# A one-core attention and expert kernel: three more filler matmuls, the last copies in another order, and each expert weight loaded in four column pieces

## The chip, the cores and the metric

The kernel runs on one core of a Trainium2 chip. Its engines are TensorE (PE, matrix multiplication), VectorE (DVE), ScalarE (ACT), GpSimd (POOL) and SyncE (SP, which here only issues DMAs). The metric is device time in microseconds, the median of several executions. Beside these there is one profiled execution, whose trace gives the time of every instruction and, in windows, the clock that PE was granted (1.00 is full speed).

## The reference, cut to what matters

The input is an image of 256 channels on 48 x 48 positions, that is 2304 tokens. Two layers run over it, each with a residual. The second half of layer 1 is the part that the change touches.

```python
# layer 0: group norm, then softmax attention over 2304 tokens x 4 heads in one sequence of 9216
x = x + conv_attn(group_norm(x))          # softmax(q k^T / 8) v, q/k/v: 9216 x 64
# layer 1
t = tokens(x)                              # 2304 x 256
t = t + slice_attn(layer_norm(t))          # 64 slices, 8 heads
t = t + ffn(layer_norm(t))
out = image(t)                             # back to 1 x 256 x 48 x 48

def ffn(xf):                               # 8 experts, each token goes to 2 of them
    top_w, top_i = top_k(xf @ Wg + bg, 2);  top_w = softmax(top_w)
    w_dense = sum(one_hot(top_i, 8) * top_w[..., None], axis=1)
    for e in range(8):
        h = gelu(xf @ W1[e] + b1[e])       # 256 -> 1024
        out = out + w_dense[:, e:e+1] * (h @ W2[e] + b2[e])   # 1024 -> 256
    return out
```

## The kernel before, in words

**Order of the whole.** Layer 0's attention takes the first 1211 us and isn't touched. Slice attention follows, to about 1248 us; then routing, to about 1277 us; then the expert tiles, to about 1568 us; then the end, which adds the last tile and writes the output. A second copy of all layers stands behind a condition at the end of the program; it handles rare inputs and is not run here. It is built from the same function, `layers(tc, bad, ...)` with `bad=None`.

**What sets the order.** `pe`, `dve`, `act`, `pool` and `sp` are wrappers (`InOrder`, L65 to 76) that keep every instruction on its engine in the order in which it is written; since the wrapper issues them, most instructions carry line 73 in the profile and are told apart by the names of their tiles. Between engines a framework puts in semaphores: a reader waits for the writer of the part of a tile that it reads, and a writer of a buffer waits until its last readers are done. Indirect DMAs on POOL are kept in written order by `indirect` (L1314 in the profile). DMAs of W1 are issued by SP directly (L1354).

**Routing (L1120 to L1266).** DVE computes each token's two experts and its slot: tokens are sorted by expert and cut into tiles of 128 slots, each tile of one expert. To invert the map (which token sits in a slot?) PE multiplies one-hot matrices: `find_rows(k, n)` has DVE write n one-hot planes and PE accumulate n matmuls of 43 columns into `pw`. There are 36 of them, in groups of 6, 12, 12 and 6. Between the groups PE waits for DVE. The transpose `pex` brings out the expert of each tile. `pq` then spreads the positions for gathers in quarters. Where PE would have nothing to do, `busy(n, bank)` (L458) issues n matmuls of 256 columns whose result nobody reads (`spin<-Wqkv_sb,ident` in the profile; each fp32 matmul leaves two records). Thirteen of them stand before the one-hot groups, three after them and seven at the end. The very next PE work then waits for the first gather of tokens.

**Expert tiles.** There are 39 tiles here: first tiles 36, 37 and 38 (`near`), then 0 to 35 (`SURE` is 36); further ones (`rare`) are not run. For tile s:

- `parts` or `rows` gathers its 128 token rows with indirect DMAs on POOL, three tiles ahead; `turn` or `turn_parts` transposes them into `xT`.
- `load_w1(s, w1)` (L1352) reads the tile's expert number into an SP register and loads the whole W1 of that expert, 1 MB, into one of two buffers of 128 partitions x 2 x 1024. It stands two tiles ahead: the load of s+2 is issued after `first(s)`, and since it writes the buffer that `first(s)` reads, it waits for `first(s)` to be done.
- `first(s)` (L1401) makes 16 matmuls into `ph`: for each of the eight blocks f of 128 hidden columns two (c = 0, 1) over the two halves of the 256 inputs, with `w1[:, c, f*128 : (f+1)*128]` as PE's weights. ACT applies gelu block by block.
- `second(s)` (L1419) multiplies with W2, which lies in SBUF (`w2_sb`): 8 matmuls into `py`; DVE adds the bias and multiplies with the routing weight (`y`). `first` of a tile stands ahead of `second` of the tile before.
- `scatter` adds y to the tokens `t_d` in DRAM by an indirect DMA on POOL.

**The end (L1599 to L1634).** The 2304 output tokens are cut into five blocks: 0 and 1 (tokens 1792 on and 1280 on, 512 each, `EARLY`), which the last two tiles cannot reach, are loaded while these tiles run; 2 (768, 512 tokens), 3 (0, 512) and 4 (512, 256) are loaded after the last scatter (`LATE`). For each block and each half c of the channels, `columns(b, c)` transposes on PE into a PSUM bank out of the ring of three `ph` banks; `finish(b, c)` (L1534) copies it to SBUF: c = 0 on DVE, c = 1 on ACT, followed by the block's output DMA, issued by ACT for blocks 0, 1 and 4 and by SP for the others. A bank can be written again only when its copy is done. The last tile, 35, is not scattered: DVE splits its y into three bf16 parts (`thirds`, five DVE instructions), and PE adds them to the blocks 2 to 4 by three one-hot matmuls (`here`) on top of the transposes. In the order of before, the copies of block 0 stand after `second(35)` and those of block 1 after the split into `thirds`.

Of the kernel before, what the change touches and what calls it, by code (L numbers as in the profile page):

```python
# [18 lines left out]
P = 128  # L19
# [15 lines left out]
HID = 1024  # L35
# [43 lines left out]
def layers(  # L79
# [10 lines left out]
    nc = tc.nc  # L90
# [3 lines left out]
    pe, dve, act, pool = (InOrder(tc, e) for e in (nc.tensor, nc.vector, nc.scalar, nc.gpsimd))  # L94
# [18 lines left out]
        out=not_before, in_=not_before, pattern=[[-1, P]], compare_op=ALU.is_ge,  # L113
# [69 lines left out]
    for c, pieces in enumerate(((1152, 1152), (1152, 768, 384))):  # L183
# [10 lines left out]
        out=gmat, in_=gmat, pattern=[[-8, 16], [0, 8]], compare_op=ALU.is_ge,  # L194
# [3 lines left out]
        out=gmat, in_=gmat, pattern=[[8, 16], [0, 8]], compare_op=ALU.is_ge,  # L198
# [37 lines left out]
    def load_rows(src, n, name):  # L236
        t = const.tile([P, 2, n], FP, name=name)
        nc.sync.dma_start(out=t, in_=src.rearrange("(c p) n -> p c n", p=P))
        return t
# [3 lines left out]
    Wqkv_sb = load_rows(Wqkv, 3 * C, "Wqkv_sb")  # L243
# [3 lines left out]
    for h in range(H1):  # L247
        at = ((h // 2) % 2 * 2 + h // 4) * D1
        nc.sync.dma_start(
            out=Wout_sb[at : at + D1, h % 2, 0:C], in_=Wout[h * D1 : (h + 1) * D1, :]  # L250
# [38 lines left out]
    with proj, tc.tile_pool(name="ps_pj", bufs=5, space=PSUM) as ps_pj, tc.tile_pool(  # L289
# [147 lines left out]
        for i in range(NTT):  # L437
            pv = ps_pj.tile([P, 512], FP, name="pp", tag="pp")
            for c in range(2):
                nc.tensor.matmul(  # L440
                    pv[:, 0:C], xn[:, c, i * P : (i + 1) * P], WvT[:, c, :],
                    start=(c == 0), stop=(c == 1),
# [15 lines left out]
    def busy(n, bank):  # L458

        for _ in range(n):  # L460
            pe.matmul(bank[:, 0:256], ident, Wqkv_sb[:, 0, 0:256], start=True, stop=True)
# [146 lines left out]
    def attention():  # L608
# [220 lines left out]
    spin = idle.enter_context(tc.tile_pool(name="ps_spin", bufs=1, space=PSUM)).tile(  # L829
        [P, 256], FP, name="spin"  # L830
    )
# [27 lines left out]
    for c in range(2):  # L859
        pe.matmul(  # L860
            pts[:, c, :], sums_of[:, c * P : (c + 1) * P], fold.rearrange("p a s -> p (a s)"),
            start=(c == 0), stop=False,
# [10 lines left out]
    for ci in range(2):  # L873
        for k in range(2):
            pe.matmul(
                gates[:, ci, :], turned[:, k, ci * P : (ci + 1) * P], Wl[:, k, S : S + E],
                start=(k == 0), stop=(k == 1),
            )
    for k in range(2):
        pe.matmul(  # L880
            gates[:, 2, :], bcol[:, B_OUT + k : B_OUT + k + 1].to_broadcast([P, P]), Wl[:, k, S : S + E],
            start=(k == 0), stop=(k == 1),
# [3 lines left out]
    for c in range(2):  # L886
        for i in range(NTT - 2, NTT):
# [3 lines left out]
                start=False, stop=(c == 1 and i == NTT - 1),  # L891
# [25 lines left out]
    with tc.tile_pool(name="sa", bufs=1) as sa, sums_done, tc.tile_pool(  # L917
# [10 lines left out]
        with tc.tile_pool(name="ps_b", bufs=3, space=PSUM) as ps_b:  # L928
# [5 lines left out]
            for m in range(2):  # L934
                for c in range(2):
                    pe.matmul(
                        ph[:, m, :], W0_sb[:, c, m * P : (m + 1) * P], ts_sum[:, c * S : (c + 2) * S],
                        start=(c == 0), stop=(c == 1),
# [28 lines left out]
            for u in range(2):  # L967
                ph = ps_b.tile([P, 2, 2 * S], FP, name="ph", tag="mm")
                phs.append(ph)
                for kind in range(2):  # L970
                    j = 2 * kind + u
                    for c in range(2):
# [3 lines left out]
                            start=(c == 0), stop=(c == 1),  # L976
# [57 lines left out]
            pt = ps_b.tile([P, 2, S], FP, name="pt2", tag="mm")  # L1034
# [8 lines left out]
            for w in range(2):  # L1043
                pe.matmul(
                    pw, tokT[:, w].rearrange("p a s -> p (a s)"), Wout_sb[:, w, :],
                    start=(w == 0), stop=(w == 1),
# [23 lines left out]
        with tc.tile_pool(name="ps_y0", bufs=1, space=PSUM) as ps_y0:  # L1070
# [3 lines left out]
            for g, (i0, n) in enumerate(groups):  # L1074
                pys = [next(banks)[:, 0 : C + E] for _ in range(n)]
                for i in range(i0, i0 + n, 4):
                    some = range(i, min(i + 4, i0 + n))
                    for k in some:
# [4 lines left out]
                            stop=(k < 4 or k in by_dve),  # L1083
# [4 lines left out]
                for k, py in enumerate(pys):  # L1088
# [16 lines left out]
                    out=t_d[(i0 + 1) * P : (i0 + n + 1) * P, :].rearrange("(i p) c -> p i c", p=P),  # L1105
                    in_=t_sb[:, these, 0:C],
# [13 lines left out]
    with gating, tc.tile_pool(name="onehot", bufs=1) as oh, tc.tile_pool(  # L1120
# [68 lines left out]
        for k in range(2):  # L1189
# [4 lines left out]
            out=tn_d[P : P + NT, C : C + E].rearrange("(i p) e -> p i e", p=P), in_=w_e  # L1194
# [15 lines left out]
        dve.scalar_tensor_tensor(row, first_slot, -BIG, slot, ALU.add, ALU.subtract)  # L1210

        which = oh.tile([P, NSL, K], HF, name="which")
        in_row = t_flat.bitcast(HF)[:, 0 : P * K].rearrange("p (r k) -> p r k", k=K)
        in_tile = t_flat.bitcast(HF)[:, P * K : (P + NSL) * K].rearrange("p (n k) -> p n k", k=K)
        pw = ps_lg.tile([P, NSL], FP, name="pw")
        pex = ps_lg.tile([1, P], FP, name="pex")
        busy(13, spin)
        tokens = token.rearrange("p k i -> p (k i)")
        dve.tensor_tensor(
            in_tile, tile_of.unsqueeze(1).to_broadcast([P, NSL, K]), tile_tab, ALU.is_equal  # L1220
        )
        def weigh(k):
            ks = slice(k, k + NTT)
            dve.tensor_tensor(
                which[:, :, ks], in_tile[:, :, ks],
                tokens[:, ks].unsqueeze(1).to_broadcast([P, NSL, NTT]), ALU.mult,
            )

        def find_rows(k, n):
            dve.tensor_tensor(  # L1230
                in_row[:, :, k : k + n], row[:, k : k + n].unsqueeze(1).to_broadcast([P, P, n]),
                row_tab[:, :, k : k + n], ALU.is_equal,
            )
            for j in range(k, k + n):
                pe.matmul(pw, in_row[:, :, j], which[:, :, j], start=(j == 0), stop=(j == K - 1))
# [6 lines left out]
        dve.tensor_reduce(ex, past, AX.X, ALU.add)  # L1242
        dve.tensor_copy(used_i, ends[0:1, E - 1 : E])
        pe.transpose(pex, ex, ident)
        find_rows(6, 12)
        dve.tensor_copy(expert_i, pex[:, 0:NSL])
        weigh(NTT)
        find_rows(NTT, 12)
# [19 lines left out]
    def expert_of(s, engine):  # L1268
        return nc.values_load(
            expert_i[:, s : s + 1], engines=(engine,), min_val=0, max_val=E - 1,  # L1270
            skip_runtime_bounds_check_because="it is counted from 0 and cut at E - 1",
        )

    idle.close()
    with tc.tile_pool(name="ps_h", bufs=1, space=PSUM) as ps_h, tc.tile_pool(
# [75 lines left out]

        def load_w1(s, w1):  # L1352
            e = expert_of(s, mybir.EngineType.SP)
            nc.sync.dma_start(  # L1354
                out=w1, in_=W1[bass.ds(e, 1)].rearrange("e (p c) f -> p (e c) f", p=P)
            )
            return w1

        def behind(ins, last):
# [59 lines left out]
        def second(s, hid, meanwhile):  # L1419

            e = expert_of(s, mybir.EngineType.PE)
            py = next(ring_py)
            for f in range(NHC):
                pe.matmul(
                    py, hid[:, f, :],
                    w2_sb[:, bass.ds(e, 1), f, :].rearrange("p e d -> p (e d)"),
                    start=(f == 0), stop=(f == NHC - 1),
                )
                if f == 2:
                    meanwhile()  # L1430
            e = expert_of(s, mybir.EngineType.DVE)
            y = next(ring_y)
            dve.tensor_tensor(
                y, py, b2_e[:, bass.ds(e, 1), :].rearrange("p e d -> p (e d)"), ALU.add
            )
            dve.tensor_scalar(y, y, slot_w.pop(s), None, ALU.mult)
            return y
# [14 lines left out]
        xs, w1, xT, hid, slot_w = {}, {}, {}, {}, {}  # L1452
        for s in near:
            xs[s] = rows(s, next(near_xs))
        for s in range(2):
            w1[SURE + s] = load_w1(SURE + s, next(ring_w1))
# [31 lines left out]
        turn_next(SURE)  # L1488
        hid[SURE] = first(SURE, xT.pop(SURE), w1.pop(SURE))
        w1[SURE + 2] = load_w1(SURE + 2, next(ring_w1))  # L1490
        scatter(SURE, second(SURE, hid.pop(SURE), more_turns))
        used = nc.values_load(
# [22 lines left out]
        blocks, pts, ob_of = [], {}, {}  # L1515
# [8 lines left out]
        def columns(b, c):  # L1524
            t0, n, tt = blocks[b]
            pts[b, c] = next(ring_ph).rearrange("p a b -> p (a b)")
            by_row = pts[b, c][:, 0:n].rearrange("q (p k) -> q k p", p=P)
            for k in range(n // P):
                pe.matmul(
                    by_row[:, k, :], tt[:, k, c * P : (c + 1) * P], ident, start=(k == 0),  # L1530
                    stop=(t0 >= reach and k == n // P - 1), is_transpose=True,
                )

        def finish(b, c):  # L1534
            t0, n, _ = blocks[b]
            pt = pts.pop((b, c))
            if c == 0:
                ob_of[b] = next(obs)
                dve.tensor_copy(ob_of[b][:, c, 0:n], pt[:, 0:n])
            else:  # L1540
                act.copy(ob_of[b][:, c, 0:n], pt[:, 0:n])

                queue = act if t0 in (1792, 1280, 512) else sp
                queue.dma_start(out=out_v[:, :, t0 : t0 + n], in_=ob_of.pop(b)[:, :, 0:n])
# [3 lines left out]
        for s in range(SURE):  # L1548
# [41 lines left out]
            if 8 <= s < 8 + len(TBLOCKS):  # L1590
                t0, n = TBLOCKS[s - 8]
# [9 lines left out]
        if bad is not None:  # L1601
            columns(0, 0)
            columns(0, 1)
        y = second(SURE - 1, hid.pop(SURE - 1), lambda: None)
        if bad is not None:
            columns(1, 0)
            finish(0, 0)
            finish(0, 1)
            columns(1, 1)
            busy(2, next(ring_py))  # L1610
        else:
            busy(4, next(ring_py))
# [4 lines left out]
        dve.tensor_copy(thirds[:, 2], rest[:, 1])  # L1617
        first_late = 0
        if bad is not None:
            finish(1, 0)  # L1620
            finish(1, 1)
            first_late = 2
        todo = [(b, c) for b in range(first_late, len(blocks)) for c in range(2)]
        columns(*todo[0])
        for at, (b, c) in enumerate(todo):
            if at + 1 < len(todo):
                columns(*todo[at + 1])
            t0, n, _ = blocks[b]
            for k in range(3 if t0 < reach else 0):
                pe.matmul(  # L1630
                    pts[b, c][:, 0:n], thirds[:, k, c * P : (c + 1) * P], here[:, t0 : t0 + n],
                    start=False, stop=(k == 2),
# [4 lines left out]
@with_exitstack  # L1637
def kernel(ctx: ExitStack, tc: tile.TileContext, *args):
    nc = tc.nc
    out_v = args[-1][0].rearrange("(c p) h w -> p c (h w)", p=P)  # L1640
    known = ctx.enter_context(tc.tile_pool(name="known", bufs=1))
    bad = known.tile([1, 1], mybir.dt.int32, name="bad")
    ident = known.tile([P, P], FP, name="ident")
    make_identity(nc, ident)
    dram = ctx.enter_context(tc.tile_pool(name="t", bufs=1, space=bass.MemoryType.DRAM))
    t_d = dram.tile([NT + P, C], FP, name="t_d")
    layers(tc, bad, ident, t_d, out_v, *args[:-1])

    flags, (again,) = nc.values_load_multi_w_load_instructions(
        bad, min_val=0, max_val=1, skip_runtime_bounds_check_because="it is the result of a comparison"  # L1650
    )
    for flag in flags:
        tc.keep_in_program_order(flag)
    with tc.If(again > 0):
        layers(tc, None, ident, t_d, out_v, *args[:-1])
# [35 lines left out]
```

## Time and profile before

| what | us |
|---|---|
| median of 3 runs (lowest to highest) | 1576.4 (1575.71 to 1576.87) |
| the profiled execution's own time | 1585.12 |
| its span in the trace | 1583.4 |
| PE busy, of the span | 1558.1 (98%) |
| DVE busy | 1051.8 (66%) |
| ACT busy | 820.9 (52%) |
| POOL busy | 264.9 (17%) |
| mean granted PE clock of the profiled execution | 0.995 |

The profile is of one execution, and it took 8.7 us longer than the median of the runs. A share of busy time is an average over stages; what bounds a stage is read from the stage itself, by the idle time before a group and by what ended it (in brackets, with an arrow from the instruction that was waited for). In a line of a group, the tiles are written as result<-operands, then partitions x elements and the type, then how many instructions there are. A fp32 matmul leaves two or more records; counts of records are not counts of calls. Times in the trace are counted from the start of the span.

### The profile page before, as it was taken

The numbers are of one execution on the slowest core, as the hardware profiler recorded it, in microseconds if no ns is written. First come the engines' busy times: TensorE is split into PE (matmuls) and PEld (weight loads), VectorE is DVE, ScalarE is ACT, GpSimd is POOL, SyncE is SP. The second block draws the span as 40 slices with busy tenths as digits, with TensorE's granted clock in tenths as the row PEclk, the third lists the DMA queues.
The fourth block names the chain that finished last, engine by engine and source line by source line (L and its number), as shares of the span: only waits on it lengthen the run. The fifth ranks groups of instructions, "written<-read, shape, count | busy, mean of one in ns | idle before, by whom it ended". The sixth has DMA issues, their size and how long they took to land. (4 is left out here: it accounts for less than half of the span.)

```text
span 1583.4 us, 32366 instructions
## 1 busy us (share of the span) xinstructions
PE 1558.1 (98%) x13058; PEld 775.6 (49%) x13059; DVE 1051.8 (66%) x1430; ACT 820.9 (52%) x1132; POOL 264.9 (17%) x206
## 2 busy tenths in 40 slices
PE   9999999999999999999999999999999999999997
PEld 5633343333333333333333333333334788899986
DVE  7578777787787877878778778777787712222222
ACT  3356665565665665556556656566654423233322
POOL 1101101011011010110100101101010145656661
PEclk9999999999999999999999999999999989999999
DMA  4000000000000000000000000000001956666656
GB/s 142 2 1 1 1 1 4 5 1 1 8 1 1 8 1 1 8 2 1 6 4 1 2 7 1 1 8 1 1 2 45 317 172 188 169 179 190 180 168 185
DMA packets 57214, 80.08 MB, mean 51 GB/s; under 512 B 27375, under 2 KB 47550, under 8 KB 51934
## 3 DMA queue, kind: packets, MB, share of 16 engines
q1 hardware_dynamic: 47026, 66.01, 12.8%
q0 software_dynamic: 9104, 10.53, 3.7%
q8 instruction: 107, 1.75, 0.5%
q10 hardware_dynamic: 924, 1.35, 0.2%
q14 instruction: 53, 0.43, 0.1%
HBM read 63.37 MB, written 12.40 MB: 48 GB/s over the span
## 5 line engine op out<-in xcount | busy, mean ns | idle before, releaser
L73 DVE TENSOR_TENSOR acc<-acc,p 128x1024 f32<-128x1024 f32 x612 | 749.2, 1224 | 242.7 <-ACT p L73 236.9
L73 ACT ACTIVATE p<-s 128x1024 f32<-128x1024 f32 x648 | 662.8, 1023 | 469.7 <-PE s L73 467.2
L73 PE MATMUL av<-p,v_sb 64*64 64x512 f32 x5184 | 675.8, 590 | 2.5 <-ACT p L73 1.4
L73 PE MATMUL s<-q,kk 64*64 64x512 f32 x5184 | 674.8, 589 | 0.5 <-DVE v_sb L444 0.5
L73 PEld LDWEIGHTS s<-q,kk 64*64 64x64 f32 x5184 | 202.1, 133 | 353.5 <-issue 181.5
L73 PEld LDWEIGHTS av<-p,v_sb 64*64 64x64 f32 x5184 | 195.7, 131 | 358.0 <-ACT p L73 201.1
L73 POOL PARTITION_ALL_REDUCE total<-both x17 | 71.5, 4206 | 954.8 <-ACT p L73 893.4
L73 ACT ACTIVATE hid<-ph,bcol 128x128 f32<-128x128 f32 x312 | 88.8, 369 | 215.4 <-PE ph L73 121.6
L73 PE MATMUL ph<-xT,w 128*128 128x128 f32 x1248 | 146.8, 275 | 4.0 <-issue 1.7
L73 PE MATMUL py<-w_sb,hid 128*128 x624 | 146.9, 383 | 2.9 <-issue 2.5
L73 PEld LDWEIGHTS ph<-xT,w 128*128 128x128 f32 x1248 | 145.8, 192 | 6.8 <-ACTq L1505 2.1
L73 DVE TENSOR_TENSOR y<-py,b_bc 128x256 f32<-128x256 f32 x39 | 16.6, 425 | 172.0 <-PE py L73 102.6
L73 PEld LDWEIGHTS py<-w_sb,hid 128*128 128x128 f32 x624 | 115.3, 192 | 19.4 <-issue 5.2
L1314 POOL DMA_INDIRECT xs<-tn_d,part_t x88 | 90.0, 1023 | 33.6 <-issue 25.9
L1314 POOL DMA_INDIRECT t_d<-y,slot_t x36 | 57.8, 1605 | 78.6 <-DVE xT L73 28.0
L73 DVE COPY xT<-pt 128x256 f32<-128x256 f32 x17 | 7.2, 423 | 50.1 <-PE pt L73 47.1
L73 DVE RECIPROCAL rinv<-rinv 128x256 f32<-128x256 f32 x17 | 29.7, 1745 | 0.0
L73 POOL TENSOR_TENSOR rstd_t<-ve,mhalf 128x2 f32<-128x2 f32 (+2 forms) x13 | 11.0, 848 | 103.4 <-DVE ve L73 96.5
L73 DVE TENSOR_TENSOR acc<-p 128x1024 f32<-128x1024 f32 x18 | 22.8, 1268 | 4.7 <-ACT p L73 3.1
L395 DVE TENSOR_SCALAR q<-pp,bcol 64x512 f32<-64x512 f32 (+1 forms) x30 | 20.8, 694 | 5.0 <-PE pp L378 4.7
L73 DVE TENSOR_REDUCE up<-av 128x512 f32<-128x1024 f32 x17 | 20.8, 1225 | 5.0 <-PE av L73 5.0
L73 PE MATMUL spin<-Wqkv_sb,ident 128*128 128x256 f32 x88 | 24.1, 430 | 0.0
(325 smaller groups left out, 612.6 us busy)
## 6 DMA issues: line engine op xcount, KB each, us to landing
w<-in_L_ffn_W_dram SPq DMA_DIRECT2D x39, 1024.0 KB
w_sb<-in_L_ffn_W_dram SPq DMA_DIRECT2D x8, 1024.0 KB
t_sb<-turned SPq DMA_DIRECT2D x224, 8.0 KB
t_sb<-t_d SPq DMA_DIRECT2D x4, 512.0 KB
x_sb<-in_x_dram SPq DMA_DIRECT2D x3, 576.0 KB
t_d<-t_sb SPq DMA_DIRECT2D x2, 768.0 KB
tn_d<-tn SPq DMA_DIRECT2D x2, 768.0 KB
xs<-tn_d,part_t POOLq DMA_INDIRECT x88
```

Source lines behind the costliest of these rows:

```text
L73: return self.tc.keep_in_program_order(getattr(self.engine, name)(*args, **kwargs))
L395: nc.vector.tensor_scalar(dst, pq[rows, 0:tn], bcol[rows, B_Q + m : B_Q + m + 1], 0.125, ALU.add, ALU.mult,)
L1314: new = nc.gpsimd.indirect_dma_start(**kwargs)
```

## The change

Three things are edited.

- In routing, three fillers are added, each between two one-hot groups: `busy_half()`, new, a matmul of 128 columns, after the thirteen fillers; one `busy(1)` of 256 columns after the transpose `pex`; and a second `busy_half()` after the group `find_rows(6, 12)`.
- `load_w1` issues four DMAs instead of one. Each takes a quarter of the hidden columns (256 of 1024) of both input halves, for all 128 partitions, so that a run in memory is 1 KB and there are 256 runs for each DMA. Each piece waits only for the readers of its own columns, and `first` waits for each piece at f = 0, 2, 4 and 6.
- At the end, `finish(0, 0)` and `finish(0, 1)` go ahead of `second(35)`. After it come `columns(1, 0)` and `columns(1, 1)`, then `finish(1, 0)`, now copied by ACT, and `finish(1, 1)`; all these stand ahead of the split into `thirds`.

The fallback copy gets the fillers and the W1 pieces too, and isn't run.

```diff
         pex = ps_lg.tile([1, P], FP, name="pex")
         busy(13, spin)
+        busy_half()          # pe.matmul(spin[:, 0:P], ident, Wqkv_sb[:, 0, 0:P], start=True, stop=True)
         tokens = token.rearrange("p k i -> p (k i)")
...
         pe.transpose(pex, ex, ident)
+        busy(1, spin)
         find_rows(6, 12)
+        busy_half()
         dve.tensor_copy(expert_i, pex[:, 0:NSL])
...
             e = expert_of(s, mybir.EngineType.SP)
-            nc.sync.dma_start(
-                out=w1, in_=W1[bass.ds(e, 1)].rearrange("e (p c) f -> p (e c) f", p=P)
-            )
+            for f0 in range(0, HID, HID // 4):
+                fs = slice(f0, f0 + HID // 4)
+                nc.sync.dma_start(
+                    out=w1[:, :, fs],
+                    in_=W1[bass.ds(e, 1)].rearrange("e (p c) f -> p (e c) f", p=P)[:, :, fs],
+                )
             return w1
...
-        def finish(b, c):
+        def finish(b, c, by=None):
...
-                dve.tensor_copy(ob_of[b][:, c, 0:n], pt[:, 0:n])
+                (dve.tensor_copy if by is None else act.copy)(ob_of[b][:, c, 0:n], pt[:, 0:n])
...
             columns(0, 1)
+            finish(0, 0)
+            finish(0, 1)
         y = second(SURE - 1, hid.pop(SURE - 1), lambda: None)
         if bad is not None:
             columns(1, 0)
-            finish(0, 0)
-            finish(0, 1)
             columns(1, 1)
+            finish(1, 0, act)
+            finish(1, 1)
             busy(2, next(ring_py))
...
         dve.tensor_copy(thirds[:, 2], rest[:, 1])
         first_late = 0
         if bad is not None:
-            finish(1, 0)
-            finish(1, 1)
             first_late = 2
```

More of the change, by code (lines that the diff above doesn't have):

```diff
@@ L1212, in layers, with busy_half @@
         which = oh.tile([P, NSL, K], HF, name="which")
+        def busy_half():
+            pe.matmul(spin[:, 0:P], ident, Wqkv_sb[:, 0, 0:P], start=True, stop=True)
         in_row = t_flat.bitcast(HF)[:, 0 : P * K].rearrange("p (r k) -> p r k", k=K)
```

## Prediction

> **What bounds the kernel now.** I read the page first, then the clock and busy time by stretch, the order of time at the three places that the change touches, and the weight loads.
>
> ```profile
> PE 1558.1 (98%) x13058; PEld 775.6 (49%) x13059; DVE 1051.8 (66%) x1430; ACT 820.9 (52%) x1132; POOL 264.9 (17%) x206
> PE   9999999999999999999999999999999999999997
> PEclk9999999999999999999999999999999989999999
> ```
>
> TensorE (PE) is the bound almost everywhere: 25 us of the span are not matmul, 7 of them after the last matmul. Only idle PE, or PE at a low clock, can be won. The one 8 in the row of the granted clock lies at the routing stage, between attention and the expert tiles. By stretches of 3.41 us (start and end, length, then the engines, the clock after POOL):
>
> ```profile
> 1259.15:1262.56 3.41, 3.41 (x17) 2.87 (x16) 3.24 (x8) 1.89 (x3) 0.51 (x1) 1.00 0.89 251
> 1262.56:1265.97 3.41, 2.27 (x22) 1.57 (x21) 3.38 (x10) 0.00 (x0) 0.00 (x0) 1.00 0.20 18
> 1265.97:1269.39 3.42, 3.42 (x23) 3.06 (x24) 1.50 (x7) 0.00 (x0) 0.00 (x0) 0.50 0.71 244
> 1272.80:1276.21 3.41, 3.41 (x10) 2.69 (x9) 0.00 (x0) 0.00 (x0) 2.77 (x3) 0.50 0.39 107
> 1310.35:1313.76 3.41, 1.76 (x10) 1.26 (x9) 1.50 (x7) 1.14 (x4) 1.14 (x2) 1.00 0.40 94
> 1382.03:1385.44 3.41, 1.78 (x6) 0.78 (x5) 1.86 (x8) 0.00 (x0) 2.80 (x3) 1.00 0.40 89
> ```
>
> PE runs at 0.50 from 1265.97 to 1276.21. The work in that stage, in order of time (start, length; in brackets the idle time before):
>
> ```profile
> 1263.21 0.68 PE L73 MATMUL pw<-which,t_sb 128*128 128x43 f16 x6 [0.40 <-DVE t_sb L73]
> 1263.71 0.29 PE L73 MATMUL pex<-ident,ex 128*1 128x128 f32 x1
> 1264.46 1.18 PE L73 MATMUL pw<-which,t_sb 128*128 128x43 f16 x12 [0.46 <-DVE t_sb L73]
> 1265.92 1.68 PE L73 MATMUL pw<-which,t_sb 128*128 128x43 f16 x18 [0.28 <-DVE t_sb L73]
> 1267.42 2.88 PE L73 MATMUL spin<-Wqkv_sb,ident 128*128 128x256 f32 x6
> 1270.09 1.77 PE L73 MATMUL pq<-empties,quad 128*128 128x43 f32 x8
> 1271.66 5.51 PE L73 MATMUL spin<-Wqkv_sb,ident 128*128 128x256 f32 x14
> 1277.01 0.40 PE L73 MATMUL pt<-ident,near_xs 128*128 128x128 f32 x2
> ```
>
> The end of the kernel, VectorE (DVE) and PE:
>
> ```profile
> 1569.14 0.68 DVE L73 COPY w<-ph 128x512 f32<-128x512 f32 x1
> 1571.52 1.28 DVE L73 COPY w<-ph 128x512 f32<-128x512 f32 x2
> 1569.88 0.66 PE L73 MATMUL ph<-ident,t_sb 128*128 128x128 f32 x4 [1.07 <-DVE w L73]
> 1572.26 1.53 PE L73 MATMUL ph<-ident,t_sb 128*128 128x128 f32 x12 [0.42 <-DVE w L73]
> ```
>
> PE stands 1.07 and 0.42 us there for two PSUM copies that DVE makes late. Last the loads of W1 (shortest, median and longest issue), and two stretches of heavy loading: W2 in runs of 1 KB, then W1 in packets of 8 KB (the last two numbers are DMA share and GB/s):
>
> ```profile
> L1354 SPq DMA_DIRECT2D w<-in_L_ffn_W_dram x39: 332/333/382, 1265.7 to 1546.3; - x39
> 1223.00:1238.00 15.00, 14.19 (x111) 10.57 (x112) 7.01 (x26) 3.22 (x13) 0.00 (x0) 1.00 1.07 379
> 1268.00:1272.00 4.00, 4.00 (x15) 3.55 (x14) 0.91 (x6) 0.00 (x0) 1.87 (x2) 0.50 1.01 426
> ```
>
> **The end (finish moved).** Block 0's copies go ahead of the last expert matmul, where DVE has been idle for 7.1 us and ScalarE (ACT) makes its half already at 1565.16. Its output DMA, now issued at 1569.90, then goes at about 1565.9. Block 1's first half moves from DVE to ACT (about 0.59 us by the other ACT copies), ahead of ACT's own copy at 1570.57 and its DMA; ACT was idle for 4.8 us before that. So DVE's split of y into `thirds` starts 0.5 us earlier (1569.2, not 1569.74) and ends near 1571.05, not 1571.60; block 2's copy follows at once, at 1571.05 and not 1572.12. On PE, (1,1) no longer waits (1.07), and the next blocks start near 1570.0. From block 2's second half on PE has 4.0 us of work (1572.26 to 1576.32); it can start at 1570.4, and waits some 0.45 us for DVE's copy of block 2 (buffer back at 1571.73) and some 0.2 for the loads: PE ends near 1575.1, that is 1.2 us earlier, and with it the last output. The early output takes 512 KB of DMA time (1.4 us at its packets' rate, 86 ns for 2 KB on 16 engines) from the three late token loads in flight from 1566.0 to 1570.7; that could push the last to about 1572, where PE needs it at 1572.8. Range of the end: -0.5 to -1.5; taken -1.2.
>
> **The fillers.** Two halves (two records of 128 columns, 0.22 us) and one whole (two of 256, 0.43 us), each in a gap of the lines above: 0.40, 0.46 and 0.28 us. All three fit, so their cost is nothing; without the cover 0.87 us. What they can win is the clock. Without the drop the first six spins take 1.3 us, `pq` starts at 1268.9 (`empties` is ready by then), and the last 14 end near 1272.8. Then PE waits for the first gather, whose last packets end at 1273.1 in the trace: PE's next work moves from 1277.0 to 1273.2, 3.8 us.
>
> Does the drop go? The row is not explained by idle time: the longest gap was 0.46 us. The Trainium skill ("TensorE: Matmul & The Clock Gate", "Why this matters for your kernels") asks authors to avoid PE gaps over about 3 us; by that rule there was nothing to lose here, and fillers in gaps of 0.4 us win 0. Another section of that page ("A second HAM failure mode") tells of one kernel whose very short idles between groups of matmuls brought the clock down; no size is given. The row decides: the stage lost its clock with PE "busy" for 2.27 of 3.41 us, because the 43-column matmuls stream for 18 of the 98 ns between them. Counting only streaming time (0.42 ns per half-precision column, 0.87 per fp32 column, from the pace of repeated matmuls), windows had these shares: 0.155 before this drop, 0.32 at 1382.03 (also dropped), 0.43 at 1310.35 (held). The threshold lies between 0.32 and 0.43. The fillers add 0.85 us, 0.25 of a window: 0.405 here, inside that gap. The windows of 3.41 us (the rows' 10.24 and 3.41 us at half clock are 3 and 1 of them) are free-running by the same page's Part 1, so I slid their grid over the rebuilt stage: before, the lowest share lies at 0.14 to 0.41 by phase; after, at 0.33 to 0.53. For thresholds of 0.33 to 0.40 the drop occurs in 83 to 100% of phases before and in 22 to 64% after, and the mean gain is 1.0 to 1.35 us. Taken -1.3; ends 0 and -3.9.
>
> **W1 in four pieces.** One DMA of 128 runs of 8 KB becomes four of 256 runs of 1 KB. Per tile SP issues four instead of one (three times 0.33 us and a register move more), with nothing else in its queue than the next load. POOL's gathers are not passed. PE waits four times per tile instead of once, and signals each quarter. Transfer: 1.05 MB at 379 instead of 426 GB/s, 2.8 instead of 2.5 us. It hides behind PE's 7.03 us per tile: from the trace's landings, each load before was complete 1.7 to 8.6 us ahead of its first matmul, so an earlier start frees nothing on the path. The PE waits: weight loads of `ph` with a semaphore wait stand 112 ns after the one before, those without one also 112. Nothing, then; but where the skill's fit of about 2.0 us fixed per DMA ("DMA: Bandwidth & Descriptors", "Anatomy of one DMA", made for POOL's path) is taken as serial, four pieces cost 4 x (2.0 + 0.6) = 10.4 us, over PE's 7.03: +120 us in all. The row says no: W2's eight DMAs ran back to back at 379 GB/s, the fixed part overlapped. Gathers start late under a burst of W1 (packets of 1357 wait until 1360.0 in the trace), and shorter bursts can only help them; their data is used a tile later. Taken 0, ends -3 and +12.
>
> **Sum.** -1.2 - 1.3 + 0 = -2.5 us. The profiled execution took 1585.1 us (span 1583.4, 1.7 around it), the median is 1576.4. The 8.7 us between them are about what PE loses in stalls of the expert stage with no cause in the program (4.4 us idle, 1.65 before 1313.3, 1.7 at half clock after 1385): I take these to belong to the profiled run, and count no gain on them. The terms carry over: 1576.4 - 2.5 = 1573.9.
>
> **The rivals.**
> - The clock holds in nearly every run (threshold near 0.33): -1.2 - 3.6 = 1571.6. For it: no filler fits worse than its gap; against: 0.405 is inside the unknown range.
> - The fillers do nothing, because the threshold is above 0.42 or the timed runs never dropped: 1575.2. For it: the three timed runs lie within 1.2 us although phases should scatter them by more.
> - The stalls are in the timed runs too, and shorter bursts of W1 take away half of them: -2.5 - 3 = 1570.9. For it: the stall at 1360 ends when a W1 load lands; against: that at 1311.9 does not.
> - Slower: the three new waits per tile keep weight loads from being pulled ahead, one load of 0.11 us each: 117 waits, +12.9, with the gains 1586.8. It decides from 0.05 us per wait (5.7 us in all). Against: the 112 ns above.
>
> **How the numbers follow.** The forecast has 0.40, the rivals 0.22, 0.15, 0.10 and 0.13. Bound of "no change": 0.2%, 3.2 us, about what a measurement here can tell. Faster than 1573.2: the clock case and the stalls case nearly whole, and a good quarter of the forecast's spread (1571.5 to 1575.5): 0.41. Slower: 0.14. Within: 0.45. Range 1570.0 to 1580.0: it takes in all but the far side of the slow case and the deep end of the clock and stall cases.
>
> **What would show it.** The clock row at 1.00 through routing, PE's `pt<-ident,near_xs` right after the gather; no wait on DVE's copies at the end and the last ACT copy 1.2 us after less; PE pace of `ph` unchanged at 3.57 us per tile, with W1 complete well before use. A `ph` group longer than 3.57 us, or waits on W1, makes it wrong.

## The result, and the profile after

The changed kernel took 1593.1 us (median of 3 runs, 1586.19 to 1598.44); the kernel before 1576.4 (1575.71 to 1576.87). The ratio is 1.0095, with a 95% interval of 1.0072 to 1.0118: the change made the kernel slower. The forecast was 1573.9, with a range up to 1580.0.

The page of the changed kernel, busy times and the rows of PE and of its clock:

```profile
PE 1558.6 (98%) x13065; PEld 777.4 (49%) x13065; DVE 1051.6 (66%) x1429; ACT 821.2 (51%) x1133; POOL 264.9 (17%) x206
PE   9999999999999999999999999999999899999997
PEclk9999999999999999999999999999999999999999
```

PE's busy time grew by 0.5 us only (1558.1 to 1558.6), the span by 13.2 us (1583.4 to 1596.6). The time is in gaps of PE and at half clock.

Routing and the first expert tile, in stretches of one clock window (start and end, length, busy time of PE, PEld, DVE, ACT, POOL, clock, DMA share, GB/s):

```profile
1261.91:1265.32 3.41, 3.22 (x22) 2.45 (x21) 3.34 (x9) 0.00 (x0) 0.00 (x0) 1.00 0.52 81
1265.32:1268.73 3.41, 3.40 (x35) 3.15 (x34) 2.09 (x5) 0.00 (x0) 0.00 (x0) 1.00 0.23 69
1272.15:1275.56 3.41, 1.31 (x7) 0.81 (x5) 0.00 (x0) 0.00 (x0) 2.80 (x3) 1.00 0.92 279
1275.56:1278.97 3.41, 2.18 (x9) 1.82 (x10) 0.58 (x2) 0.00 (x0) 2.24 (x3) 0.50 0.60 197
1278.97:1282.39 3.42, 3.42 (x18) 3.42 (x18) 0.00 (x0) 1.10 (x4) 0.00 (x0) 0.50 0.38 116
```

The clock now holds through routing, which the fillers were meant to reach, and is lost at 1275.56. The order of time says why:

```profile
1264.49 0.59 PE L73 MATMUL spin<-Wqkv_sb,ident 128*128 128x256 f32 x2
1266.10 0.44 PE L73 MATMUL spin<-Wqkv_sb,ident 128*128 128x128 f32 x2
1270.19 3.27 PE L73 MATMUL spin<-Wqkv_sb,ident 128*128 128x256 f32 x14
1276.27 0.68 PE L73 MATMUL pt<-ident,near_xs 128*128 128x128 f32 x2 [2.81 <-DMA near_xs<-tn_d,from_t]
```

The fillers run, the last spins end at 1273.46, and then PE stands 2.81 us for the first gather. That gather's data is used at 1276.27; in the trace of before its packets were in at 1273.1. So the window up to 1275.56 is mostly empty, and the next two run at 0.50.

In the run of tiles, two lines of the operations on the W1 buffers (shortest, median and longest of a group):

```profile
L73 PE MATMUL ph<-xT,w x1248: 269/275/582, 1277.5 to 1577.6; 128*128 128x128 f32 x179
L1362 SPq DMA_DIRECT2D w<-in_L_ffn_W_dram x156: 314/543/1297, 1266.3 to 1560.2; - x156
```

The median `ph` matmul is as before (275 ns). An issue of a piece takes SP 0.54 us, where one whole load took 0.33: a tile's four are 2.2 us of SP. The waits of PE in that stage (total, how many, longest):

```profile
PE ph L73 <- issue: 14.7, 20, 1.1
PE ph L73 <- ACTq L1514: 1.8, 1, 1.8
```

20 times PE stood in front of a `ph` matmul, 14.7 us in all, without a wait that the profile could name (it writes "issue"). Before, it was 1.7 us there and 2.5 us at `py`, by the page of before:

```profile
L73 PE MATMUL ph<-xT,w 128*128 128x128 f32 x1248 | 146.8, 275 | 4.0 <-issue 1.7
L73 PE MATMUL py<-w_sb,hid 128*128 x624 | 146.9, 383 | 2.9 <-issue 2.5
```

The line with ACTq is the branch around the tiles that are not run. Two of the 20 places, PE first, then what POOL was doing:

```profile
1403.46 3.62 PE L73 MATMUL py<-w_sb,hid 128*128 x16
1406.91 1.42 PE L73 MATMUL ph<-xT,w 128*128 128x128 f32 x10
1409.28 0.49 PE L73 MATMUL ph<-xT,w 128*128 128x128 f32 x3 [0.95 <-issue]
1410.72 2.28 PE L73 MATMUL ph<-xT,w 128*128 128x128 f32 x19 [0.95 <-issue]
```

```profile
1402.72 1.62 POOL L1320 DMA_INDIRECT t_d<-y,slot_t  x1 [0.30 <-issue]
1404.64 1.06 POOL L1320 DMA_INDIRECT xs<-tn_d,part_t  x1 [0.30 <-issue]
1406.00 1.01 POOL L1320 DMA_INDIRECT xs<-tn_d,part_t  x1 [0.31 <-issue]
1407.32 1.01 POOL L1320 DMA_INDIRECT xs<-tn_d,part_t  x1 [0.30 <-DMA t_d<-y,slot_t]
```

Last the end of the kernel, PE:

```profile
1583.87 1.06 PE L73 MATMUL ph<-ident,t_sb 128*128 128x128 f32 x8
1586.63 1.06 PE L73 MATMUL ph<-ident,t_sb 128*128 128x128 f32 x8 [1.70 <-DMA t_sb<-t_d]
```

The waits for copies (1.07 and 0.42 us) are gone; one of 1.70 us for a late token load has come. From the start of the last tile's `second` PE needs 11.60 us to its end, before 11.55.

**When the W1 loads are issued.** The time at which SP issues a load of W1 can be set against the later of two times: the end of the matmul that it waits for, and the end of SP's own step before it. Normally the issue is 0.03 us behind. An issue more than 0.3 us behind is called late here:

| kernel | W1 issues that wait for PE | late | sum of lateness, us | longest, us |
|---|---|---|---|---|
| before, profile shown ahead of the prediction | 37 | 16 | 46.9 | 4.8 |
| changed, first result | 148 | 40 | 72.6 | 3.6 |

The trace also records when the counter (semaphore) that PE raises for SP and others goes up, and this shows that the signal itself is late, not SP. All 16 late issues of before follow a recorded increment by 0.02 us. In the changed trace, around the stretch shown above, eleven increments fall due between 1400.05 and 1408.11 by the ends of their matmuls. One is recorded at 1403.97, one at 1407.72, seven in a burst from 1410.73 to 1411.09, and two have no record. PE, which has stood twice for 0.95 us, goes on at 1410.72. At 9 of the 20 places PE goes on within 0.1 us of the start of such a burst. That PE stands because its signals cannot leave is inferred from this, not shown.

All 40 late issues, and 15 of the 16, fall where POOL is issuing a gather or a scatter. By itself that says little: in five traces with one load per tile and no late signal, 34 of the 37 signals fall there as well. These were the conditions of the first result; the experiments below met them once more, in one set of six.

### The profile page after: what moved, and what is told of

It is laid out like the page before. It is cut to its first block, busy times and chain, and to the rows that moved or that the text cites. A ratio compares the mean times of both kernels' runs of the same rounds, so it can differ in the third digit from the quotient of the medians.

```text
span 1596.6 us, 32879 instructions
## 1 busy us (share of the span) xinstructions
PE 1558.6 (98%) x13065; PEld 777.4 (49%) x13065; DVE 1051.6 (66%) x1429; ACT 821.2 (51%) x1133; POOL 264.9 (17%) x206
## 5 line engine op out<-in xcount | busy, mean ns | idle before, releaser
L73 PE MATMUL ph<-xT,w 128*128 128x128 f32 x1248 | 153.6, 279 | 16.7 <-issue 14.7
L73 PEld LDWEIGHTS ph<-xT,w 128*128 128x128 f32 x1248 | 150.8, 195 | 21.5 <-issue 17.2
L73 PE MATMUL spin<-Wqkv_sb,ident 128*128 128x256 f32 (+1 forms) x94 | 21.7, 378 | 0.0
```

The lines of the kernel that those rows point to most:

```text
L73: return self.tc.keep_in_program_order(getattr(self.engine, name)(*args, **kwargs))
```

## The experiments

The kernels were run in six sets. Those of one set ran on the same chip and share its runs of the kernel before, so each is compared with that. Medians in us.

### The parts one by one (kernel before: 1573.4)

W1 in pieces alone (the diff's hunk in `load_w1`, nothing else):

> The kernel before with W1 in four column pieces and nothing else. Theory A (the pieces make the whole loss): 1586 to 1596 us, 10 to 20 above before, with PE standing still in steps of about 0.7 us inside the ph matmuls and SP's issues late while GpSimd makes gather descriptors. Theory B (the loss comes from the pieces together with the fillers, by the first gather that lands late and the clock that drops after it): under 1581.

Measured 1576.98, ratio 1.0023 (1.0015 to 1.0031): +3.6. No issue was late, and PE did not stand in `ph`. Of the two theories the second has its number (under 1581), but only half its cause: the first gather does come late and the clock drops after it, without any fillers. The pieces lose by themselves, and far less than in the first result. PE's waits for the first gather and at the branch, in its trace:

```profile
1276.44 0.48 PE L73 MATMUL pt<-ident,near_xs 128*128 128x128 f32 x2 [1.87 <-DMA near_xs<-tn_d,from_t]
...
1313.75 3.81 PE L73 MATMUL ph<-xT,w 128*128 128x128 f32 x32 [1.75 <-PEq L1508]
```

The changed kernel without the pieces:

```diff
-            for f0 in range(0, HID, HID // 4): ...
+            nc.sync.dma_start(out=w1, in_=W1[bass.ds(e, 1)].rearrange("e (p c) f -> p (e c) f", p=P))
```

> The changed kernel with W1 loaded whole again. Theory A: no slower than before; with the sums of the prediction 1573.9, and with the end worth nothing (the changed profile has 14.7 us from the last scatter to PE's end, as before) about 1574.5 to 1576. Theory B also gives this. If the moved copies at the end cost time, 1578 or more.

Measured 1571.2, ratio 0.9989 (0.9983 to 0.9996): -2.2. In a later set it was 1571.37 beside 1572.81, ratio 0.9989 (0.998 to 0.9999).

> The changed kernel with W1 whole: 1 to 3 us under the kernel before, whether signals come late or not, since neither end nor fillers add a signal from PE to SP.

The three fillers alone:

> The kernel before with the three fillers alone. Prediction's term: -1.3 us (between 0 and -3.9), so about 1575, with the granted clock at 1.00 through routing and the first transpose of gathered tokens at about 1273.5 in the trace. If the timed runs never lost the clock: 1576.4.

Measured 1572.22, -1.2 by the medians; the ratio, 0.9996 (0.9988 to 1.0005), doesn't tell it from nothing. The granted clock of each run tells more. Of the 53 runs of the kernel before, 25 had a mean clock of 0.995 or 0.996 and took 1574.8 on average, 24 had 0.998 or more and took 1571.9. With the fillers all 13 runs had 0.998 or more; a loss of three windows, as in the first profile of before, would take 0.003 off the mean. The two stretches that matter in its trace, both at 1.00:

```profile
1263.04:1266.46 3.42, 3.20 (x28) 2.40 (x28) 3.39 (x10) 0.00 (x0) 0.00 (x0) 1.00 0.19 17
1266.46:1269.87 3.41, 3.41 (x31) 3.18 (x31) 1.45 (x7) 0.00 (x0) 0.00 (x0) 1.00 0.76 257
```

The end alone:

> The kernel before with the copies and the output of blocks 0 and 1 moved, and nothing else. Prediction's term: -1.2 us, 1575.2. By the changed profile (PE waits 1.70 us for a token load in place of 1.49 us for copies) 0: 1576.4.

Measured 1573.22, ratio 0.9998 (0.9989 to 1.0006): no difference to be seen. In its trace PE ends 10.98 us after the last `second` starts, 0.57 less than before; such a gain is below what these runs can tell.

### The change again, and three kinds of load (kernel before: 1573.23)

> The changed kernel once more, beside its parts on the same chip. In the first result it took 1593.1, with PE standing in steps of 0.7 us inside the ph matmuls; the pieces alone took 1576.98 beside 1573.4 for the kernel before, with no such step in their trace. Theory A (the parts add up: end and fillers -2.2, pieces +3.6): 1 to 2 us above the kernel before. Theory C (the three parts together make the standing times): 10 to 20 above.

Measured 1577.63, ratio 1.0026 (1.0017 to 1.0034): +4.4, with no issue late; in the stretch that follows each increment of PE's counter is recorded 0.02 us after its matmul. First the same tile turn as above, without a stop, then all of PE's waits from the first tiles to the end of the tiles:

```profile
1397.17 3.62 PE L73 MATMUL py<-w_sb,hid 128*128 x16
1400.62 3.73 PE L73 MATMUL ph<-xT,w 128*128 128x128 f32 x32
1404.19 3.62 PE L73 MATMUL py<-w_sb,hid 128*128 x16
```

```profile
PE ph L73 <- PEq L1514: 2.2, 1, 2.2
PE ph L73 <- DMA t_sb<-t_d: 1.7, 1, 1.7
```

So of the first result's +16.7 only 4.4 return where signals come in time.

Pieces, but whole loads for the first two tiles:

```diff
+            if SURE <= s < SURE + 2:
+                nc.sync.dma_start(out=w1, in_=...)      # whole
+                return w1
```

> The kernel before with W1 in four column pieces, but the loads of the first two tiles (36 and 37) whole. Theory G (the pieces cost by the first gather, which waits behind eight slowly issued loads of W1 and lets PE stand and the clock drop): as the kernel before, within 1 us. If the pieces cost per tile (waits on PE, a slower pace of ph): 3 us or more above before, as with all loads in pieces (+3.6).

Measured 1575.52, ratio 1.0018 (1.0008 to 1.0028): +2.3. Better than all loads in pieces, and not yet the kernel before: the first gather is a part of the cost.

Pieces in reverse order, `reversed(range(0, HID, HID // 4))`, so that the first one issued waits for the last matmul:

> The kernel before with W1 in four column pieces, the last columns first, so that all four loads are issued only when the whole tile before is done; PE still waits for four pieces. If the early start of single pieces costs (transfers spread over ph): near the kernel before, under +1.5. If the number or the kind of the loads costs, or the first gather behind them: +3 to +4, as with all pieces in order.

Measured 1577.51, ratio 1.0025 (1.0016 to 1.0035): +4.3. The early start is not what costs.

One load, runs of 1 KB (a gap of 8 columns after each 256 in the buffer, `fp.tile([P, 8 * 264], ...)`):

> The kernel before with one load per W1 tile, but in runs of 1 KB (the buffer has a gap after every 256 columns). If the small runs cost (transfer 2.8 in place of 2.5 us, and the first gather behind them): +2 to +4. If the four issues cost and not the runs: as the kernel before, within 1 us.

Measured 1573.81, ratio 1.0002 (0.9993 to 1.0011): no difference. By the medians small runs alone don't cost; splitting the load does.

### Where the pieces cost (kernel before: 1573.61, then 1573.14)

The time from POOL's issue of the first gather to PE's first use of it, and PE's wait at the branch, each from one trace:

| kernel | W1 issues ahead of the gather's end | last W1 packet after the gather's issue, us | gather issued to used, us | wait at the branch, us |
|---|---|---|---|---|
| fillers alone | 2 | 3.0 | 3.9 | 0.9 |
| without pieces | 2 | 3.8 | 4.6 | 0.8 |
| first two loads whole | 2 | 3.7 | 4.5 | 1.6 |
| pieces alone | 8 | 6.8 | 6.0 | 1.8 |
| changed, second run | 8 | 7.1 | 6.0 | 2.2 |
| changed, first result | 8 | 6.9 | 5.8 | 1.8 |

In the third row PE was busy with fillers until it used the gather, so 4.5 is an upper bound there. The gather shares the DMA engines with W1 of tiles 36 and 37. In eight pieces these leave SP only by 1.6 us after the gather is issued (1272.04 against 1270.45 in the changed trace), so the gather is in the midst of them.

At the branch the loads of tiles 2 and 3 are in flight, and there the small transfer that comes late is code. In all 16 traces with signals in time PE goes on 2.0 to 2.2 us after the end of a 16 KB packet of an instruction queue (q8 in the page; that it carries PE's program is inferred from its 1.75 MB). This packet starts 0.5 to 1.1 us after PE's last `py` group does where these two loads are whole and in runs of 8 KB (seven traces). It starts 1.3 to 2.4 us after where they are split in order (six traces). If these two places are all, whole loads at both should end the cost:

```diff
+            if s in (SURE, SURE + 1, 2, 3):
+                nc.sync.dma_start(out=w1, in_=...)      # whole
+                return w1
```

> The kernel before with W1 in four column pieces, but whole for tiles 36 and 37 (ahead of the first gather) and for tiles 2 and 3 (in flight at the branch around the tiles that are not run). If these two places are all that the pieces cost where PE's signals come in time: as the kernel before, within 1 us. If the pieces cost in the run of tiles too: 2 us or more above it.

Measured 1573.02, ratio 0.9996 (0.9987 to 1.0005): the cost is gone, with 35 tiles still in pieces. The granted clock of the runs goes with it. Its mean was 0.9958 with pieces alone (before, in the same set: 0.9969), 0.9960 with the first two loads whole (before: 0.9970), and 0.9972 with four whole (before: 0.9969).

The same four whole loads in the complete change:

> The changed kernel whole, fillers, end and pieces, but with whole loads of W1 for tiles 36, 37, 2 and 3. If the first gather and the branch are all that the pieces cost where PE's signals come in time: 2 us under the kernel before, as with no pieces at all (1571.2 beside 1573.4). If the fillers or the end lose by the pieces elsewhere: level with before or above. If PE's signals come late on this chip: 5 us or more above before, with SP's issues late.

Measured 1570.97, ratio 0.9988 (0.9981 to 0.9994): -2.2, the gain of the version without pieces. First gather and branch in the changed kernel (its third run), then with four whole loads, each in order of time:

```profile
1271.29 3.27 PE L73 MATMUL spin<-Wqkv_sb,ident 128*128 128x256 f32 x14
1275.83 0.47 PE L73 MATMUL pt<-ident,near_xs 128*128 128x128 f32 x2 [1.27 <-DMA near_xs<-tn_d,from_t]
...
1308.81 2.75 PE L73 MATMUL py<-w_sb,hid 128*128 x12
1313.56 3.81 PE L73 MATMUL ph<-xT,w 128*128 128x128 f32 x32 [2.00 <-DVEq L1514]
```

```profile
1271.07 3.27 PE L73 MATMUL spin<-Wqkv_sb,ident 128*128 128x256 f32 x14
1274.18 0.40 PE L73 MATMUL pt<-ident,near_xs 128*128 128x128 f32 x2
...
1305.45 2.76 PE L73 MATMUL py<-w_sb,hid 128*128 x12
1309.10 3.81 PE L73 MATMUL ph<-xT,w 128*128 128x128 f32 x32 [0.89 <-DVE y L73]
...
1558.29 1.06 PE L73 MATMUL ph<-ident,t_sb 128*128 128x128 f32 x8 [0.48 <-DMA t_sb<-t_d]
```

With four whole loads no wait stands before `pt`, and the wait at the branch is 0.89 in place of 2.00. This version and the one without pieces are the best measured, 0.1% under the kernel before; the pieces add nothing to it.

The changed kernel's third run, beside the version with four whole loads in the kernel before:

> The changed kernel a third time, to see on which chips PE's signals to SP come late. If they come in time as in its second run: 3 to 6 us above the kernel before. If they come late as in its first run, and as in the first profile of the kernel before: 10 to 20 above, with SP's issues of W1 late by up to 3 us behind PE.

Measured 1577.62, ratio 1.002 (1.0009 to 1.0032): +4.0, no issue late.

W1 in two pieces (`HID // 2`):

> The kernel before with W1 in two column pieces (two loads of 512 KB, runs of 2 KB). If the number of issues ahead of the first gather sets the cost (four in place of two, where the changed kernel has eight): between the kernel before and +2.5 us, about +1.2. If any split at all costs the whole: +3 to +4.

Measured 1577.89, ratio 1.0029 (1.0021 to 1.0037): +4.8, as much as four. The gather came to use 6.1 us after its issue, as with eight issues, although SP had started the last of its four issues 1.3 us before the gather. So the expected step by the number of issues is not there. One load in runs of 1 KB had 5.9 us in its trace, but that trace is of its slowest run (1576.28), and in the median it lost nothing. What in a split load holds up the gather and the code packet is left open.

### Where signals come late (kernel before: 1583.27)

> The changed kernel a fourth time. If PE's signals come in time on this chip: 3 to 6 us above the kernel before. If they come late: 10 to 20 above.

Measured 1595.65 (five runs), ratio 1.0078 (1.0039 to 1.0116): +12.4, and the kernel before was itself 10 us above its other sets. 38 of 148 issues were late, by up to 3.8 us (69.5 in sum), and each fell beside a gather or scatter of POOL. It is like the first result. The chip has the same number as that of two sets without late signals, so the chip alone does not decide it. In the same set, with every gather of tiles 2 to 35 in quarters (`return 2 <= s < SURE` in `in_parts`):

> The changed kernel with all gathers of tiles 2 to 35 in quarters (four DMAs each, where every third tile had one), so that GpSimd issues 36 more. If GpSimd's descriptor work alone makes PE's signals late: more than 20 of the 148 W1 issues late by over 0.3 us, and 5 us or more above the changed kernel. If it is the chip: at most 5 late, and the time within 5 us below the changed kernel or level (PE is spared 11 pairs of transposes, about 0.46 us each).

Measured 1621.76 (two runs), ratio 1.0235 (1.0199 to 1.0271): 26 above the changed kernel. 58 of 148 issues were late (116.2 us in sum). PE's waits:

```profile
PE ph L73 <- issue: 24.9, 40, 1.2
PE ph L73 <- ACTq L1514: 6.5, 1, 6.5
```

With more descriptor work on POOL more signals were late and PE stood more often. The expectation's first branch has its numbers, but this kernel was not run where signals come in time, so how much of the 26 us belongs to lateness is open. POOL's work is not enough by itself: in the second run of the changed kernel 107 of the 148 signals came while POOL was issuing, in time. A further factor, which these kernels don't set, decides whether there is lateness at all.

One candidate is untested: the recording of the trace. Nearly every time on record comes from an execution with a recorded span and clock. In the four profiles with late signals, and in no other, many semaphore records are missing: of the 1077 or 1078 increments of ACT's counter 980 to 1009 are there, elsewhere all. Whether the recording takes part in the lateness or only suffers from the same cause, no run shows.

A last set was meant to part the two further, with row gathers only (`in_parts` false), whole loads and pieces, and the reverse order once more:

> The kernel before with every tile gathered in one indirect DMA, none in quarters; PE then has 23 more pairs of transposes, about 0.23 to 0.46 us each. If PE's signals come in time here: 5 to 11 us above the kernel before. If they come late in this call, and it is GpSimd's descriptor work that makes them late: less above than that, or under the kernel before, with fewer than 5 of 37 issues late.

> The same with W1 in four column pieces. If the meeting of pieces and quarter gathers costs: at most 5 us above the kernel with row gathers and whole W1 (first gather and branch), also where signals come late. If the pieces cost by themselves there: 10 us or more above it.

> The kernel before with the four pieces in reverse order, all issued when the tile before is done. Where signals come late: if every piece that waits on PE adds its own late signal, far under the pieces in order, at most 6 above the kernel before; if the number of loads beside the gathers counts, 10 or more above. Where they come in time: +4.

The signals came in time in this set (kernel before 1572.81), so it says nothing on lateness. Row gathers cost +5.9 (1578.75, four runs, ratio 1.0037, 1.0019 to 1.0055). With pieces it was 1584.43, 5.7 more and a little above the 5 that were allowed, from three runs between 1580.86 and 1584.85. In reverse order it was 1576.56, ratio 1.0026 (1.0017 to 1.0036), +3.8.

## Why the prediction was wrong

It failed at two terms that it put at nothing: "W1 in four pieces", taken as 0, and the stalls of the expert stage, on which the sum counted nothing.

**The pieces at the first gather and at the branch.** "POOL's gathers are not passed" and "an earlier start frees nothing on the path" looked at the run of tiles, where each load has microseconds of slack; the runs with signals in time bear that out, since 35 tiles in pieces cost nothing. But the loads of tiles 36 and 37 are in flight with the first gather, for which PE waits, and those of tiles 2 and 3 with the code that PE needs after the branch. There the split loads hold up what PE waits for. The clause "shorter bursts can only help them" was wrong for the first gather: it came to use 5.3 to 6.2 us after its issue beside split loads. Beside whole loads it was 3.9 to 4.7 us, wherever PE was ready for it (5.9 in the one trace of whole loads in runs of 1 KB). Already 3.9 is more than the 3.4 us that the prediction's sum has (1269.83 to 1273.2). It read "whose last packets end at 1273.1" from the trace of before and kept it as a constant in the sum of the fillers, although the same change rearranged what shares the engines with the gather.

Of the +3.6 of the pieces alone, about 1.7 is the granted clock (0.9969 to 0.9958 over all runs, times 1574 us). The rest, some 2 us, agrees with the two longer waits in single traces: the gather in use 1.4 us later than without pieces (6.0 against 4.6), and PE's wait at the branch longer by 0.6 to 1.0 us. The split is an estimate, since 4.6 comes from a kernel with fillers. In the traces of before and of the end alone, which lost three clock windows, PE itself came later than the gather (7.2 and 7.0 us after its issue, without a wait).

**The stalls.** "I take these to belong to the profiled run, and count no gain on them", said of the stalls of the expert stage, is the larger error. It held for the three timed runs of before, but it put at nothing what the change would add where signals are late. The trace of before already had SP issuing 16 of its 37 loads up to 4.8 us late. The change makes four waits on such a signal out of one, and 40 of them were late. In the expert stage PE's idle time went from 6.4 to 16.8 us, and the time with the clock at half from 3.4 to 8.3 us. A rival had these stalls, but with the sign turned: shorter bursts were to relieve them.

Of the first result's +16.7, some 4 are the two places above, by the sets with signals in time (+4.0 and +4.4). The rest comes only where signals are late: +12.4 in the late set, where the kernel before is late as well. But the three timed runs of before in the first result (up to 1576.87) lie where its runs in time lie (1570.3 to 1577.0) and not with the late ones (1582.2 to 1588.4). So the 4 us between +16.7 and +12.4 may be the state of those runs and not the change. The upper end of +12 that the prediction gave the pieces comes near these numbers by luck, since it stood for waits on PE's weight loads; and the range cut it off.

**The slow rival.** Weight loads that are no longer pulled ahead were to cost 0.11 us per wait. The `ph` group of a tile takes 3.73 us in the changed trace, as before, and four whole loads end the whole cost while 105 of the 117 new waits stay. That mechanism is not there.

**The fillers.** -1.3 was forecast and -1.2 is the difference of medians; by its interval that is not told from nothing, so the close match is luck. The mechanism shows in the clock: the mean over the runs went from 0.9969 to 0.9981. The loss got rarer and shorter, not impossible. Of the nine traces with fillers four lose the clock in routing, each for one window of 3.41 us; of the eleven without, eight do, four of them for three windows (10.24 us), one for two and three for one. For the clock gate the row decided rightly against the rule of the Trainium skill ("TensorE: Matmul & The Clock Gate", "Why this matters for your kernels") to avoid idle gaps of PE over about 3 us: in the trace of before the longest gap was 0.46 us and the clock was lost. In the complete change the late first gather empties a later window, and the gain is spent again: all four profiles of the changed kernel lose a window that begins between 1275.4 and 1277.7, behind that wait.

**The end.** -1.2 was forecast. PE's end came 0.5 to 1.2 us earlier without pieces or with four whole loads (10.3 to 11.1 in place of 11.55 us after the last `second` starts), and the measured time of the end alone doesn't differ. The mis-sized term is the early output: the last token-load packet ends 7.6 to 7.8 us after the last `second` starts, where it was 6.0. The clause "could push the last to about 1572" was the right mechanism (7.2 on that scale); in the complete change the second late load is issued 0.27 us later than without pieces (1.34 against 1.07 us), and PE waits 1.7 to 1.9 us for the loads in all four of its traces. There the end gains nothing.

## What to carry to other kernels

A load that is hidden in the steady run of tiles may be exposed at the first tile and at every branch: cost a split or slowed transfer at these places by themselves, against whatever small transfer the first consumer waits for. Take a stall in the profile that has no cause in the program as a cost that the change may multiply; compare the time of each issue with the end of what it waits for, since this shows late signals that no list of waits names. When three edits go in together, one of them may spend what another earns, as the late gather did with the clock that the fillers had kept.

## What had not been expected of the hardware

- PE's signals came up to 4.8 us late in some sets and 0.02 us behind in others, with the same program; where they were late, the counter stood still for microseconds and then rose in a burst, some 0.04 us from one increment to the next. POOL was issuing an indirect DMA in 93 of 94 late cases (before, changed, and its fourth run), but that holds for most signals in time too. Why some sets have it stays open.
- The share of a 3.41 us window in which PE streams columns, reckoned as in the prediction, had these values nearest to the turn: 0.350, 0.355, 0.360 and 0.373 in windows that were followed by half clock, and 0.367, 0.389, 0.391, 0.392 and 0.396 in windows that were not. Single values move by some 0.03 with where in a record the streaming is placed; so reckoned, over all 20 traces the highest share that was followed by half clock is 0.40 and the lowest that was not is 0.37. The threshold, put between 0.32 and 0.43 in the prediction, lies by this estimate near 0.37 to 0.40.
- An issue of a W1 load cost SP 0.54 us with 256 runs of 1 KB or of 2 KB, 0.54 us also with 1024 runs of 1 KB in one load, and 0.33 us with 128 runs of 8 KB.
